# A decoder layer on one core: the q, k and v projections of a token group move partly into the group's own attention steps, at seven matmuls a step instead of eight

## The chip, the core and the metric

The kernel runs on one core of one Trainium2 chip. A core has five engines that run side by side, each with its own queue of instructions that it takes strictly in order: TensorE (PE, matrix multiplies and transposes, with its weight loads shown apart as PEld), VectorE (DVE), ScalarE (ACT), GpSimd (POOL) and SyncE (SP, which here only issues DMA transfers). POOL issues DMAs too. Matrix products land in PSUM, from where DVE or ACT have to copy them out to SBUF.

The metric is the device time of the whole launch in microseconds (us). Before the change it is 601.73 us, the median of three runs (600.86 to 603.8).

## The reference

Eight sequences of 256 tokens, width 512, all in float32. Attention with 16 heads of 32, a decayed running sum over a context, and a feed-forward block whose weights are splines; a layer norm after each.

```python
# attention: per sequence, 16 heads
q, k, v = heads(x @ Wq.T), heads(x @ Wk.T), heads(x @ Wv.T)
q_r, k_r, v_r = q @ Wdown, k @ Wdown, v @ Wdown        # per head, 32 x 32
attn = softmax(q_r @ k_r.T / sqrt(32))
x = layernorm(x + heads_back(attn @ v_r @ Wup) @ Wo.T)
# decayed sum over the sequence: r_t = decay * r_(t-1) + ctx_t * ctx_t
x = layernorm(x + x * r)
# feed-forward; gate_w, up_w, down_w are cubic splines of few control points
x = layernorm(x + (silu(x @ gate_w.T) * (x @ up_w.T)) @ down_w.T)
```

## The kernel before

The 2048 tokens are cut into four groups of 512 (`GT`), each of two sequences (`bb`). All that is heavy is written out by hand in one order: a wrapper (`Ordered`, L299) forces every engine to keep the order of the program. All instructions therefore carry line 308 in the profile, and are told apart by the names of their tiles.

**Start.** The weights are loaded and folded (`Wdown` into `w_q`, `Wup` and `Wdown` into `w_o`), and q, k and v of group 0 are projected in one go (L656 to L659).

**Attention.** The loop at L752 makes 32 steps, one for each group, sequence and quad of four heads. A step issues, in this order: the scores of the *next* step (`scores`, L502, eight small matmuls into four PSUM tiles `sc`), the transposes of three of its four `e` tiles (`tr_e`), two units of other work (`fill(2)`, L819), the fourth transpose, six more units (`fill`, L827), and the product with v (`weighted`, L548, tile `av`). For the next step, DVE takes the row maximum (`nmax`) and ACT the exponential (`e`); DVE and ACT in turn copy the transposes out (`eT`).

**Units.** `units` is a queue of generators with a count each; `fill(n)` (L354) advances the first one n times. A unit is mostly one matmul of 128x128 by 128x512, which the profile shows as two instructions. The kinds are: a projection of one 128-wide quarter of q, k or v of the next group (`project`, L468, four matmuls and an eviction, tiles `ps_q`, `ps_k`, `ps_v`), an output projection (`output`, L571, four matmuls, `ps_o`), and the preparation of the feed-forward inputs of a group (`inputs`, L700, eight units). At the start of a group the twelve projections of the next group join the queue (L756), all q first, then k, then v; they have to be finished before the last step of the group (L771 to L773), after which the next `xT_g` (1 MB) is loaded into the only buffer there is (L775). In the last group nothing is left to project; there `fill(2)` replaces `fill(6)`, and the inputs of the feed-forward's groups 0 and 1 are made (L758 to L760), once the pool `first` (which holds `xT_g`, `w_q`, `w_k`, `w_v`) has been closed.

**Slots.** After every second unit `fill` calls `slot()`, which advances each of the `chains` by one stage, and `some_taps()`. Chains are the layer norms (`norms`, L590, a stage on DVE, ACT or POOL per slot) and the running sum (`recur`, L486). `some_taps` (L442) adds 0.62 to a count and, when it passes one, loads the next of 57 pieces of spline taps through SP and makes weights of the piece before on POOL: six POOL operations for each of the first 16 pieces, three for the rest. The tap buffers are two, so SP waits in its queue for POOL.

**The softmax sums** of a pair of quads go through DRAM in the first three groups: a small transpose, `recT`, a DMA `rd<-recT` and a broadcast DMA `yT<-rd`, both in POOL's queue (L799, L816); DVE multiplies `yT` with `av` in the next step.

**Inputs of the feed-forward.** For a group, `inputs` transposes x2 (four units, tiles `tr_x` and `x2T`) and sends it to DRAM (`xd`, by POOL's queue); then it gathers windows of rows (`xg<-xd`, SP), multiplies with fixed moments (four units, `ps_mom`), copies these to `mom`, writes them to DRAM (`md<-mom`, POOL), and reads them back into the other rows of the same tile (`xg<-md`, SP).

**Feed-forward.** For each group, 32 gate and up products (`pg`, `pu`, `gate_up` L860) on `xg`, then the down products (`y`) and partial sums (`ps_s`). The first products of group 0 follow at once after the last attention step and read `xg` of group 0. The last output projection and its norms run inside this stage (L996, L997).

The lines that the change touches are `fill` (L354), `some_taps` (L442), `project` and `projections` (L468, L482), and the step loop (L754 to L777, L819, L827, L846).

Of the kernel before, what the change touches and what calls it, by code (L numbers as in the profile page):

```python
# [10 lines left out]
F32 = mybir.dt.float32  # L11
# [6 lines left out]
P = 128  # L18
# [3 lines left out]
DC = D // P  # L22
# [3 lines left out]
GT = 512  # L26
NG = NT // GT
# [288 lines left out]
def decoder_kernel(ctx: ExitStack, tc: tile.TileContext, x, xT, ctxT, wq, wkT, wvT, woT, wdownT, wup, decay, up_taps, down_taps, mom_f, sum_f, out, plan):  # L316
# [25 lines left out]
    first = ExitStack()  # L342
    early = first.enter_context(tc.tile_pool(name="early", bufs=1, side="right"))

    nc = Ordered(tc)
    units, chains = [], []

    def slot():

        for c in list(chains):  # L350
            if next(c, c) is c:
                chains.remove(c)

    def fill(n):  # L354

        for i in range(n):
            if units:
                next(units[0][1])
                units[0][2] -= 1
                if not units[0][2]:  # L360
                    units.pop(0)
            if i % 2:
                slot()
                some_taps()

    def norm_plain(h, s, o, other=None):

# [47 lines left out]

    folded, qkvs, rs, sums, xs, yTs = {}, {}, {}, {}, {}, {}
    dram = ctx.enter_context(tc.tile_pool(name="dram", bufs=2, space=bass.MemoryType.DRAM))

    def taps():
# [18 lines left out]
            yield  # L440

    def some_taps():  # L442
        made[0] += 0.62
        while made[0] >= 1:
            made[0] -= 1
            next(weights, None)

    weights, made = taps(), [0]
# [5 lines left out]
    def load_x(g):  # L454
        xT_g = early.tile([P, DC, GT], F32, tag="xT", name="xT_g")
        nc.sync.dma_start(out=xT_g, in_=xT[:, g * GT : (g + 1) * GT].rearrange("(c p) t -> p c t", p=P))
        return xT_g

    def evict_qkv(g, name, m, ps):
        o = qkvs[g]["qkv".index(name)][:, m, :]  # L460
        if name == "q":
            nc.scalar.mul(o, ps, scale)
        elif name == "k":
            nc.vector.tensor_copy(o, ps)
        else:
            nc.scalar.copy(o, ps)

    def project(g, name, m, xT_g):  # L468

        ps = ps_mm.tile([P, GT], F32, tag="mm", name=f"ps_{name}")  # L470
        for c in range(DC):
            if name == "v":
                lhsT, rhs = xT_g[:, c, m * P : (m + 1) * P], folded[name][:, c, :]
            else:
                lhsT, rhs = folded[name][:, c, m * P : (m + 1) * P], xT_g[:, c, :]
            nc.tensor.matmul(ps, lhsT=lhsT, rhs=rhs, start=(c == 0), stop=(c == DC - 1))
            if c < DC - 1:
                yield
        evict_qkv(g, name, m, ps)
        yield  # L480

    def projections(g, xT_g):  # L482
        qkvs[g] = group_tiles(g)
        return [[name, project(g, name, m, xT_g), DC] for name in "qkv" for m in range(DC)]

    def recur(n):  # L486

# [122 lines left out]
    w_v = early.tile([P, DC, D], F32, name="w_v")  # L610
    w_o = last.tile([P, DC, D], F32, name="w_o")
    folded.update(q=w_q, k=w_k, v=w_v)
    xT_g = early.tile([P, DC, GT], F32, tag="xT", name="xT_g")
    for c in range(DC):
        nc.sync.dma_start(out=w_k[:, c, :], in_=wkT[c * P : (c + 1) * P, :])
        nc.scalar.dma_start(out=xT_g[:, c, :], in_=xT[c * P : (c + 1) * P, 0:GT])
# [17 lines left out]
    steps = [(g, bb, quad) for g in range(NG) for bb in range(GT // T) for quad in range(NQ)]  # L634
# [20 lines left out]
        (nc.vector.tensor_copy if m % 2 else nc.scalar.copy)(w_q[:, m, :], ps)  # L655
    for name in "qv":  # L656
        for m in range(DC):
            for _ in project(0, name, m, xT_g):
                pass  # L659
    xT_g = load_x(1)  # L660
    chains.append(recur(0))
    sc = scores(0)
    es = [exponentials(0, j, sc[j]) for j in range(4)]
# [10 lines left out]
    def open_inputs():  # L674
        pool = ctx.enter_context(tc.tile_pool(name="inputs", bufs=1, side="left"))
        ffn["pool"] = pool
        ffn["mom"] = mid.enter_context(tc.tile_pool(name="mom", bufs=1, side="right"))
        ffn["mf"] = pool.tile([P, DC, 2, K2], F32, name="mf")
        nc.sync.dma_start(out=ffn["mf"], in_=mom_f)
# [71 lines left out]
    pending = None  # L751
    for s, (g, bb, quad) in enumerate(steps):  # L752
        n = g * 2 + bb
        if quad == 0 and bb == 0:  # L754
            if g + 1 < NG:
                units += projections(g + 1, xT_g)  # L756
            else:
                first.close()  # L758
                open_inputs()
                units += [["i", inputs(0), 2 * DC], ["i", inputs(1), 2 * DC]]  # L760
        if quad == 0 and n:
            load_rows(n - 1)
            o = [["o", output(n - 1, qc), DC] for qc in range(2)]
            if bb and g + 1 < NG:
                units[1:1] = o[:1]
                units.append(o[1])
            else:
                units[1:1] = o
            chains.append(recur(n))
        more = s + 1 < len(steps)  # L770
        if more and steps[s + 1][0] != g:  # L771
            while any(u[0] != "o" for u in units):
                fill(4)  # L773
            if g + 2 < NG:
                xT_g = load_x(g + 2)  # L775
        if more:
            sc = scores(s + 1)  # L777
        after = []

        def ahead(j):  # L780
# [35 lines left out]
            nc.gpsimd.dma_start(out=y.rearrange("p q t -> p (q t)"), in_=from_)  # L816
        ahead(1)
        eTs.append(evicted(tr2, nc.vector.tensor_copy))
        fill(2)  # L819
        tr3 = transposed(es[3])  # L820
        ahead(2)
        if pending is not None:
# [1 line left out]
            pending = None  # L824
        eTs.append(evicted(tr3, nc.scalar.copy))
        ahead(3)
        fill(6 if g + 1 < NG else 2)  # L827
        if quad % 2 and not short:
            tr = ps_mm.tile([P, 2, T], F32, tag="mm", name="tr_rec")
            for q in range(2):  # L830
# [14 lines left out]
    nc.scalar.activation(neghalf[:, 3:4], neghalf[:, 2:3], AF.Silu)  # L845
    for _ in weights:  # L846
        pass
    mid.close()
    load_rows(NG * 2 - 1)
    units += [["o", output(NG * 2 - 1, qc), DC] for qc in range(2)]  # L850
# [220 lines left out]
```

## Time and profile before

| what | value |
|---|---|
| time, median of three runs | 601.73 us (600.86 to 603.8) |
| the profiled execution: its span from first to last instruction | 599.9 us |
| PE busy | 573.7 us, 96% of the span |
| DVE, ACT, POOL busy | 335.5, 274.3 and 229.3 us |
| mean granted TensorE clock | 0.994 |
| 32 attention steps | from 56.9 us to 399.6 us |
| feed-forward, to the end | 399.6 us to 599.9 us |

Of the profiled execution the page gives the span alone; it stands 1.8 us under the median of the runs, which also count what lies around the first and the last instruction.

How to read it: the page first gives busy time per engine. PE is nearly always busy, so what a change can give or take is read from the places where PE is *not* busy, and from what it waits for there. A line of a timeline gives start and duration in us, engine, operation, the output tile, the input tiles, the shape, how many instructions were merged, and in brackets the idle time of the engine just before and what ended it. A line of a table by stretches gives the stretch, its length, then for each engine the busy time and the count of instructions, the granted clock, and the share and rate of the DMA engines. Ends of matmuls are modelled, and a few matmul records are missing.

### The profile page before, as it was taken

Reading aid. Unit: us, or ns where it says so; the run is one execution under the profiler, and the core shown is the slowest. Engines: PE = TensorE matmul, PEld = TensorE weight load, DVE = VectorE, ACT = ScalarE, POOL = GpSimd, SP = SyncE. Lnnn points to the kernel's source line nnn. Section 1 sums busy time; section 2 is a strip of 40 time slices with the busy share of each in tenths; the row PEclk is TensorE's granted clock in tenths of the full one; section 3 lists DMA queues with packets and bytes.
Section 4 is the critical chain, followed back from the end, with each engine's and each line's share of the span. In section 5 each row is a group of like instructions: output and inputs, shape, how many; then the busy total and the mean of one; then the engine's idle time right before and its main releaser. Section 6 shows DMA issues by size and latency. Waiting matters only on the chain.

```text
span 599.9 us, 9721 instructions
## 1 busy us (share of the span) xinstructions
PE 573.7 (96%) x3327; PEld 289.1 (48%) x3327; DVE 335.5 (56%) x741; ACT 274.3 (46%) x820; POOL 229.3 (38%) x513
## 2 busy tenths in 40 slices
PE   8999999988899999999999899999999999999993
PEld 3544545545455555555555556444344434433432
DVE  0203645558686575786664877776826505714615
ACT  0114644655655645654554677564315314504412
POOL 0000496686554535365440212200361262242253
PEclk9999999999999999999999999999999999999997
DMA  8104134335334115323210564659219987985931
GB/s 289 71 0 153 34 122 144 105 98 174 94 85 158 50 59 176 107 89 124 70 54 2 174 155 109 170 154 213 47 72 248 195 232 179 226 216 135 216 128 70
DMA packets 41696, 77.95 MB, mean 130 GB/s; under 512 B 5952, under 2 KB 10448, under 8 KB 41648
## 3 DMA queue, kind: packets, MB, share of 16 engines
q1 hardware_dynamic: 34576, 62.75, 39.8%
q0 software_dynamic: 6064, 13.41, 6.8%
q10 hardware_dynamic: 1008, 1.18, 0.7%
q8 instruction: 26, 0.43, 0.3%
q14 instruction: 22, 0.18, 0.1%
HBM read 45.22 MB, written 11.12 MB: 94 GB/s over the span
## 4 chain that ended last, share of the span: by engine, by line
PE 77%; DVE 7%; DMA 6%; POOL 5%; issue 2%; ACT 2%; POOLq 0%; SPq 0%; DVEq 0%; ACTq 0%
PE y L308 10%; PE ps_q L308 8%; PE ps_k L308 8%; PE ps_v L308 8%; PE ps_o L308 6%; PE tr_e L308 6%; PE pg L308 5%; PE ps_s L308 5%; PE av L308 5%; PE pu L308 5%; PE sc L308 4%; POOL taps L308 3%; PE ps_mom L308 2%; DMA fin<-sum 2%; DVE nmax L308 2%
## 5 line engine op out<-in xcount | busy, mean ns | idle before, releaser
L308 ACT ACTIVATE e<-sc,nmax 128x256 f32<-128x256 f32 x256 | 120.0, 479 | 76.2 <-DVE nmax L308 76.0
L308 DVE TENSOR_REDUCE nmax<-sc 128x2 f32<-128x512 f32 x128 | 85.2, 682 | 72.0 <-PE sc L308 67.0
L308 POOL TENSOR_TENSOR taps<-taps 128x256 f32<-128x256 f32 (+1 forms) x144 | 87.9, 610 | 33.8 <-DMA taps<-in_down_taps 25.8
L308 PE MATMUL tr_e<-ident,e 128*128 128x128 f32 x512 | 68.0, 276 | 0.8 <-DVE h L308 0.7
L308 PEld LDWEIGHTS tr_e<-ident,e 128*128 128x128 f32 x512 | 57.3, 140 | 22.7 <-issue 19.1
L308 PE MATMUL y<-inter,wd 32*128 32x512 f32 x512 | 63.0, 598 | 0.0
L308 PE MATMUL ps_o<-w_o,yT 128*128 128x512 f32 x128 | 60.0, 600 | 0.3 <-ACT eT L308 0.3
L308 PE MATMUL ps_v<-w_v,xT_g 128*128 128x512 f32 x128 | 58.6, 598 | 0.9 <-DVE eT L308 0.9
L308 PE MATMUL ps_k<-xT_g,w_k 128*128 128x512 f32 x128 | 58.7, 600 | 0.5 <-DMA xT_g<-in_xT 0.5
L308 PE MATMUL ps_q<-xT_g,w_q 128*128 128x512 f32 x128 | 58.2, 596 | 0.9 <-DVE eT L308 0.9
L308 ACT ACTIVATION_READ_ACCUMULATOR e<-sc,nmax 128x1 f32 x256 | 53.1, 207 | 0.0
L308 DVE TENSOR_TENSOR inter<-pu,sg 128x512 f32<-128x512 f32 x64 | 41.2, 687 | 18.3 <-PE pu L308 9.4
L308 POOL TENSOR_TENSOR rs<-va,neghalf 128x1 f32<-128x1 f32 x48 | 28.9, 602 | 49.6 <-DVE va L308 46.9
L308 ACT ACTIVATE sg<-pg 128x512 f32<-128x512 f32 x64 | 37.3, 597 | 18.4 <-PE pg L308 18.4
L308 POOL TENSOR_SCALAR va<-ss 128x1 f32<-128x1 f32 x32 | 6.5, 203 | 100.7 <-ACT x L308 51.1
L308 DVE COPY eT<-tr_e 128x512 f32<-128x512 f32 x64 | 43.8, 684 | 0.8 <-PE tr_e L308 0.7
L308 PEld LDWEIGHTS y<-inter,wd 32*128 32x128 f32 x512 | 26.7, 184 | 32.7 <-issue 27.0
L308 PE MATMUL av<-eT,v_g 128*32 128x256 f32 x512 | 36.7, 385 | 5.0 <-ACT eT L308 2.7
L308 POOL TENSOR_TENSOR r<-r 128x1024 f32<-128x1024 f32 x8 | 15.2, 1895 | 66.0 <-DMA r<-in_ctxT 65.9
L308 ACT COPY eT<-tr_e 128x512 f32<-128x512 f32 x64 | 37.3, 583 | 2.4 <-PE tr_e L308 2.4
L308 PE MATMUL sc<-k_g,q_g 32*128 32x256 f32 x512 | 37.4, 401 | 0.2 <-ACT e L308 0.2
L308 PEld LDWEIGHTS ps_v<-w_v,xT_g 128*128 128x128 f32 x128 | 23.1, 190 | 26.0 <-issue 24.3
(106 smaller groups left out, 739.8 us busy)
## 6 DMA issues: line engine op xcount, KB each, us to landing
nat<-inter SPq DMA_DIRECT2D x64, 256.0 KB
taps<-in_down_taps SPq DMA_DIRECT2D x40, 256.0 KB
taps<-in_up_taps SPq DMA_DIRECT2D x16, 384.0 KB
xg<-xd SPq DMA_DIRECT2D x8, 616.0 KB
r<-in_ctxT SPq DMA_DIRECT2D x8, 512.0 KB
x_t<-in_x SPq DMA_DIRECT2D x16, 256.0 KB
fin<-sum POOLq DMA_DIRECT2D x16, 256.0 KB, 5.3
out<-h SPq DMA_DIRECT2D x16, 256.0 KB
```

The lines of the kernel that those rows point to most:

```text
L308: return lambda *a, **k: self.tc.keep_in_program_order(f(*a, **k))
```

## The change

The projections of group g+1 are no longer bound to be finished within group g. They are queued in the order in which the steps will need them (`ORDER`: q0, k0, v0, v1, q1, k1, q2, k2, q3, k3, v2, v3), and a new function `require` advances the queue, without slots, until a named projection has been made; it is called for q and k of a step before its scores, and for two quarters of v before the product with v. Each step of the first three groups now takes seven units (2 and 5) instead of eight, each step of the last group six (2 and 4) instead of four. The number of slots is given to `fill`: one and three in a step of the first three groups, as before; one and two in the last group, where there were one and one. The count of taps grows by 0.66 a slot, not 0.62. `xT` of the next group is loaded when the last projection of a group has been evicted. The pool `first` is closed, and the preparation of the feed-forward's inputs queued, in the fifth step of the last group, not in its first. The places at which output projections enter the queue change as well. The sum of matmuls is the same.

```diff
-    def fill(n):
+    def fill(n, slots=None):
+        slots = n // 2 if slots is None else slots
         for i in range(n):
...
-            if i % 2:
+            if (i + 1) * slots // n > i * slots // n:
                 slot()
                 some_taps()
+
+    def require(g, *names):
+        while any(u[0] == (g, name) for u in units for name in names):
+            fill(1, 0)
...
+    ORDER = [(name, int(m)) for name, m in ("q0", "k0", "v0", "v1", "q1", "k1", "q2", "k2", "q3", "k3", "v2", "v3")]
...
     def some_taps():
-        made[0] += 0.62
+        made[0] += 0.66
...
-    def project(g, name, m, xT_g):
+    def project(g, name, m):
+        xT_g = xTs[g]
...
         evict_qkv(g, name, m, ps)
+        if g and (name, m) == ORDER[-1] and g + 1 < NG:
+            xTs[g + 1] = load_x(g + 1)
         yield
...
-    def projections(g, xT_g):
+    def projections(g):
         qkvs[g] = group_tiles(g)
-        return [[name, project(g, name, m, xT_g), DC] for name in "qkv" for m in range(DC)]
+        return [[(g, f"{name}{m}"), project(g, name, m), DC] for name, m in ORDER]
...
-    xT_g = load_x(1)
+    xTs[1] = load_x(1)
...
-        if quad == 0 and bb == 0:
-            if g + 1 < NG:
-                units += projections(g + 1, xT_g)
-            else:
-                first.close()
-                open_inputs()
-                units += [["i", inputs(0), 2 * DC], ["i", inputs(1), 2 * DC]]
+        if quad == 0 and bb == 0 and g + 1 < NG:
+            units += projections(g + 1)
         if quad == 0 and n:
             load_rows(n - 1)
             o = [["o", output(n - 1, qc), DC] for qc in range(2)]
-            if bb and g + 1 < NG:
-                units[1:1] = o[:1]
-                units.append(o[1])
-            else:
-                units[1:1] = o
+            at = 2 if units and (bb == 0 or units[0][2] < 2) else 1
+            units[at:at] = o[:1]
+            units[at + 2 : at + 2] = o[1:]
             chains.append(recur(n))
         more = s + 1 < len(steps)
-        if more and steps[s + 1][0] != g:
-            while any(u[0] != "o" for u in units):
-                fill(4)
-            if g + 2 < NG:
-                xT_g = load_x(g + 2)
         if more:
+            g1, _, quad1 = steps[s + 1]
+            require(g1, f"q{quad1}", f"k{quad1}")
             sc = scores(s + 1)
+        if quad == 0 and bb and g + 1 == NG:
+            require(g, *(f"{name}{m}" for name, m in ORDER))
+            first.close()
+            open_inputs()
+            units += [["i", inputs(0), 2 * DC], ["i", inputs(1), 2 * DC]]
...
-        fill(2)
+        fill(2, 1)
         tr3 = transposed(es[3])
...
-        fill(6 if g + 1 < NG else 2)
+        if g + 1 < NG:
+            fill(5, 3)
+        else:
+            fill(4, 2)
+        require(g, f"v{bb * 2}", f"v{bb * 2 + 1}")
...
     for _ in weights:
         pass
+    while units:
+        fill(2)
     mid.close()
```

## The prediction

> **What bounds the kernel now.** I read the page's busy times first, then PE by stages, then what PE waited for, then the queues that end those waits.
>
> ```profile
> span 599.9 us, 9721 instructions
> ```
>
> Stages from the table by stretches (stretch, length, then PE busy first): steps of group 0, 1, 2, 3.
>
> ```profile
> 56.87:143.88 87.01, 83.63 (x502) 44.74 (x501) 48.43 (x91) 46.80 (x165) 58.58 (x110) 1.00 0.38 118
> 143.88:236.00 92.12, 90.37 (x525) 48.00 (x525) 63.64 (x139) 50.61 (x174) 47.06 (x86) 1.00 0.37 112
> 236.00:327.80 91.80, 90.94 (x536) 48.48 (x535) 61.91 (x142) 50.49 (x172) 40.14 (x73) 1.00 0.24 74
> 327.80:399.60 71.80, 65.58 (x511) 37.52 (x510) 55.16 (x131) 46.33 (x154) 15.71 (x25) 1.00 0.56 142
> ```
>
> PE sets the pace: it is idle 3.4, 1.8, 0.9 and 6.2 us, 12.2 us in all. The change leaves PE's work as it is (in the chain of waits four projection instructions, two matmuls, take 1.72 us, so 0.86 a matmul; a step of eight units takes 11.08, one of seven 10.22). So it can win at most these 12.2 us, and loses whatever new waits it makes. The waits of PE in group 3, and the timeline around the worst one of group 0:
>
> ```profile
> PE av L308 <- DVE x2T L308: 2.3, 2, 1.2
> PE av L308 <- ACT eT L308: 1.3, 2, 1.0
> PE tr_rec L308 <- DVE mom L308: 0.8, 1, 0.8
> PE ps_mom L308 <- DVE mom L308: 0.8, 1, 0.8
> ```
> ```profile
> 123.84 0.57 POOL L308 TENSOR_TENSOR rs<-va,neghalf 128x1 f32<-128x1 f32 x1
> ...
> 124.44 0.95 DVE L308 TENSOR_SCALAR x<-h,nm,rs 128x512 f32<-128x512 f32 x1 [4.79 <-POOL rs L308]
> ...
> 126.89 1.09 PE L308 MATMUL tr_e<-ident,e 128*128 128x128 f32 x8 [0.66 <-DVE h L308]
> ...
> 128.87 1.98 PE L308 MATMUL ps_v<-w_v,xT_g 128*128 128x512 f32 x4 [0.88 <-DVE eT L308]
> ```
>
> In group 0 a norm's `rs` sits in POOL's queue behind tap work; DVE, in order, stands 4.79 us at `x`, and PE, whose transposes need PSUM that DVE should free, loses 0.66 + 0.88 = 1.54 us. Third view, POOL between its softmax DMAs, and SP and PE around the feed-forward's inputs:
>
> ```profile
> 95.21 0.74 POOL L308 DMA_DIRECT2D yT<-rd  x1 [1.92 <-DMA rd<-recT]
> ...
> 107.80 1.26 POOL L308 TENSOR_TENSOR taps<-taps 128x256 f32<-128x256 f32 x2 [2.08 <-DMA taps<-in_up_taps]
> ...
> 116.09 0.52 POOL L308 DMA_DIRECT2D rd<-recT  x1
> ```
> ```profile
> 341.79 1.53 SPq L308 DMA_DIRECT2D xg<-xd  x4
> 354.98 1.72 SPq L308 DMA_DIRECT2D xg<-md  x2
> ```
> ```profile
> 342.38 1.94 PE L308 MATMUL ps_mom<-x2T,mf 128*64 128x512 f32 x8
> ```
>
> POOL had no idle time ahead of 116.09: it is already late there. And from the last moment product of a group (344.3) to the *issue* of the read-back into `xg` pass 10.7 us.
>
> **The change, part by part.** I followed the queue by hand, counting units.
>
> *Removed.* Before, the 48 matmuls and one 8-matmul output pair of group 0 fill seven steps and the eighth has no unit: it waits 0.27 + 1.35 = 1.62 us for ACT. After, 56 units fill eight steps of seven exactly. In group 3 the four steps with outputs wait 0.35 + 0.99 + 0.29 = 1.63 us for `eT`; two more matmuls (1.7 us) cover that. Gain 3.25 us. The steps with inputs waited 4.4 us (of the 6.2) on evictions by DVE and ACT; after, these units come in rows of four as before, or denser: zero, between -1.5 and +2. The collisions of groups 1 and 2 (2.6 us): DVE has 62 us of work in 92, after 62 in 85; zero, between -2 and +2.5. Slots per step stay; in groups 0 to 2 no `require` has anything to force.
>
> *POOL in group 0.* Between the softmax DMAs of steps 3 and 5 POOL now has six pieces, not five (0.66 for 0.62; the counts reach 7.9 and 13.2), each 3.24 us (95.97 to 99.21), plus 1.9 for `r`, plus the 2.08 wait for a transfer: 23.4 us. Two shorter steps give 20.4 where they gave 22.1. Step 5 starts at 56.9 + 5x10.22 + 0.7 (the first step is longer by 0.7) = 108.7, its `rd` is wanted 2 us later, at 110.6; POOL comes free near 116.7, 6 us late (before: 1.7). Then 4.2 us of DMA pair, one piece, and `va`, `rs`: done near 125, when it was done at 124.4 before, although PE would start step 6 at 118.9 instead of 124.5. Behind the waiting DVE instruction stand `nmax` and the `eT` copies, and PE has one PSUM buffer left (`av`, `tr_r` and the begun `ps_o` hold three). Full price: 1.54 becomes 7.5, so +6. Low end: -1.5, the wait of before gone. POOL's schedule rests on one rounding and one transfer, so I take +4.5.
>
> *xT.* v3, the last of its group, is now followed closely by q0. Group 1 to 2: `tr_rec` 0.5, `av` 1.0, scores 1.1, transposes 1.5, 4.1 us in all. Group 2 to 3: four output matmuls and a transpose, 3.9. Before, the load was issued at 229.11, just after its last reader, and its 1 MB moved at 400 GB/s from 230.9 to about 233.7: 4.6 us after. Each costs 0.5 to 0.7 us, +1.2; between 0 and +3 (SP is behind POOL in its tap waits by some us in group 0).
>
> *The feed-forward's inputs.* The queue of group 3 holds 16 matmuls of projections, outputs of n = 5 and 6, then inputs(0) and inputs(1): the last start in step 29 of 0 to 31, where they started in step 24. inputs(0)'s last moment product is the fourth of six units of step 30. From there to the first gate product: two `tr_x` with a wait (1.3), `av` 1.0, and step 31 without scores: transposes 1.7, two `tr_x` with wait 1.7, `tr_e` 0.8, four moment units with wait 4.4, `tr_rec` 0.5, `av` 1.0: about 12.4 us. The gate product needs `xg` whole: copy to `mom`, POOL's `md` DMA, its landing, SP's read-back. Issue 10.7 us after the last moment product (11.1 for group 1: 381.5 to 392.6), and of that second one data moved until about 398.3, 5.7 us later: 17 us. PE stands 17 - 12.4 = 4.6; I take +4.5. Low end 0 (at the shortest `md` landing, 3.6 us, and no `xd` traffic), high end 9 (`xd` of inputs(1), 1 MB, in the same engines). Nothing else is in PE's program order there: the last output comes after the gate products. Before, 55 us of steps covered this (344.3 to 399.6).
>
> *Clock.* At the start of the span three idle products of 512, 512 and 256 columns, 2.15 us by the row above, took 4.20, so the clock was low after rest; at the end it was 1.00 in 590:592 and 0.54 in 592:594, with PE's last matmul at 590.4.
>
> ```profile
> 1.44 4.20 PE L308 MATMUL ps_idle<-idle 128*128 128x512 f32 x6 [1.44 <-DVE idle L308]
> ```
>
> So a wait of several us may cost up to 2.05 more. The longest before, 1.74, shows none (1.00). For the two long waits I take +1 each, between 0 and 2.05.
>
> Sum: -3.25 + 4.5 + 1.2 + 4.5 + 2 = +8.95 us, on a span of 599.9. The median stands 1.8 above the span, which the change doesn't touch: 601.73 + 8.95 = 610.7 us.
>
> Two rules of the Trainium skill. "DMA: Bandwidth & Descriptors", section on the anatomy of one DMA (POOL's path), puts a transfer at about 2.0 us fixed plus bytes over 436 GB/s; for the 640 KB of the write, and taken for the read-back too, that is an estimate of 3.5 us each, `xg` would be whole before PE asks, and the sum 5.5 us less, 605.2. The trace disagrees: landing of `md` has a median of 5.7 us and the read-back 5.7, in a busy queue, and I go by it. "TensorE: Matmul & The Clock Gate", Part 1, lets the clock halve after an idle window of about 3.4 us and restores it after one busy window: 1.7 us for each long wait, 3.4 for the 2 in my sum, so 612.1; the drop within 1.8 us of the last matmul fits a window that runs free.
>
> **The rivals.** (1) Only one of the two long waits comes: POOL keeps up (for: group 0 of before has 6.3 us of POOL idle at 64.3), or `xg` is whole in time (for: the shortest landing). Either way 5.5 us less: 605.2. (2) Neither comes, but the xT loads do: -3.25 + 1.2, 599.7, no change to be measured. (3) Faster: PE always has a unit at hand, so that DVE's lateness is covered in all steps and all 12.2 us of idle go; against it, the two xT loads (1.2) and the wait for `xg` (5.5 with clock) remain: 601.7 - 12.2 + 6.7 = 596.2. Its place is steps 4 to 7; it decides once POOL's lateness costs PE under about 2 us. (4) The xT load is caught in SP's queue behind a wait for POOL; SP's longest for `wu` was 13.1 us, less 4 of cover: +8 on the sum, 619.
>
> **How the numbers follow.** Forecast 0.45, with its own range of 605 to 616; one long wait only 0.25; none 0.10; faster 0.12; SP 0.08. A measurement here tells 0.5% (3 us) from no change, so under 598.7 is faster and over 604.7 slower. Slower: all but a trace of the forecast, a good half of (1), and (4): 0.66. Same: the rest of (1) and (2): 0.20. Faster 0.14. The range leaves out most of (3) below and (4) above: 598.5 to 617.
>
> **What would show it.** Right: steps of 10.2 us in groups 0 to 2; a PE wait of some us in step 6 (near 120 us) ended by DVE behind POOL's `rs`; two waits under 1 us of `ps_q` for the xT load; the first `pg` after a wait of 3 to 9 us for `xg<-md`, with a dip of the clock; the sum of PE's idle in the attention near 20 us. Wrong: no gap ahead of the first `pg`, or POOL idle ahead of step 5's `rd`. The forecast fails most easily if the transfers of `md` land fast in an emptier queue.

## The result: 650.9 us, and the profile after

The changed kernel takes 650.88 us (median of four runs, 649.03 to 653.94), against 601.39 us for the kernel before: a ratio of 1.082, with a 95% interval of 1.079 to 1.086. That is 49.5 us slower. The forecast had the sign, +9 us, and its range ended at 617. The span of the profiled execution grew as the median did, from 599.9 to 648.9 us.

The page's first lines, the kernel after:

```profile
span 648.9 us, 9726 instructions
## 1 busy us (share of the span) xinstructions
PE 583.7 (90%) x3327; PEld 296.1 (46%) x3327; DVE 335.6 (52%) x741; ACT 275.0 (42%) x820; POOL 232.4 (36%) x513
```

DVE, ACT and POOL are busy as long as before, within about 3 us. PE has the same matmuls and is still busy for 10.0 us more (583.7 for 573.7): matmuls at half clock take longer. The other 39 us are idle time of PE. The table by stretches of the kernel after, the steps of groups 0 to 3 (stretch, length, busy time of PE, PEld, DVE, ACT and POOL, granted clock, DMA share and rate):

```profile
56.70:157.90 101.20, 86.95 (x512) 46.15 (x511) 51.62 (x102) 48.63 (x171) 64.50 (x119) 0.95 0.31 97
157.90:249.70 91.80, 84.73 (x523) 45.37 (x519) 62.35 (x142) 49.89 (x172) 46.78 (x84) 1.00 0.38 118
249.70:349.60 99.90, 88.59 (x527) 46.76 (x523) 61.81 (x142) 49.96 (x172) 38.66 (x69) 0.95 0.27 77
349.60:436.70 87.10, 76.43 (x533) 42.67 (x529) 61.34 (x148) 49.80 (x159) 16.99 (x27) 1.00 0.26 74
```

Lengths have to be compared with the work that each group now holds. Those of the kernel before are taken in the same way, from the first scores issued in a group (at 56.87, 144.87, 237.03 and 328.82) to those of the next, and to the first gate product at 399.58; the prediction's stretches of groups 1 to 3 begin some 1 us earlier. Groups 1 and 2 have eight matmuls fewer than before (6.9 us at 0.86 each), group 3 has sixteen more (13.7 us).

| stage | before | after | difference | difference for the same work |
|---|---|---|---|---|
| group 0 | 88.0 | 101.2 | +13.2 | +13.2 |
| group 1 | 92.2 | 91.8 | -0.3 | +6.6 |
| group 2 | 91.8 | 99.9 | +8.1 | +15.0 |
| group 3 | 70.8 | 87.1 | +16.3 | +2.6 |
| feed-forward | 200.3 | 212.2 | +11.9 | +11.9 |

So the loss is in five places at once, and for the same work no stage gained. What PE waited for, over the whole span of the kernel after (total us, times, longest):

```profile
PE tr_e L308 <- DVE eT L308: 21.2, 21, 9.2
PE ps_s L308 <- DMA nat<-inter: 7.9, 1, 7.9
PE ps_q L308 <- DMA xT_g<-in_xT: 7.1, 2, 5.8
PE tr_e L308 <- ACT eT L308: 5.1, 7, 0.7
PE pg L308 <- issue: 3.2, 2, 2.6
```

None of these five groups came to 1 us before. Each is one mechanism, or two in the case of `tr_e`; I take them in the order of the program.

**POOL in group 0.** The timeline around step 6, POOL's softmax DMAs, the norm behind them, and PE:

```profile
120.89 0.52 POOL L308 DMA_DIRECT2D rd<-recT  x1
124.53 0.72 POOL L308 DMA_DIRECT2D yT<-rd  x1 [3.12 <-DMA rd<-recT]
128.91 0.57 POOL L308 TENSOR_TENSOR rs<-va,neghalf 128x1 f32<-128x1 f32 x1
129.51 0.94 DVE L308 TENSOR_SCALAR x<-h,nm,rs 128x512 f32<-128x512 f32 x1 [10.82 <-POOL rs L308]
131.71 1.11 PE L308 MATMUL tr_e<-ident,e 128*128 128x128 f32 x4 [9.25 <-DVE eT L308]
```

This is the chain that the prediction described, and larger: `rd` was wanted near 111.6 (an estimate: 2 us after step 5 began at 109.7) and issued at 120.89, 9 us late where 6 were forecast; DVE stands 10.82 us at `x`, PE 9.25 us behind DVE. Step 6 lasts 24.05 us.

**Steps that begin with a half-made tile.** The other `tr_e` waits are short and many. PE's timeline in step 1 and in steps 14 and 15:

```profile
68.83 1.04 PE L308 MATMUL tr_e<-ident,e 128*128 128x128 f32 x8
70.22 0.66 PE L308 MATMUL tr_e<-ident,e 128*128 128x128 f32 x4 [0.35 <-DVE eT L308]
...
226.13 0.66 PE L308 MATMUL tr_e<-ident,e 128*128 128x128 f32 x4 [0.79 <-DVE eT L308]
227.52 0.66 PE L308 MATMUL tr_e<-ident,e 128*128 128x128 f32 x4 [0.73 <-ACT eT L308]
...
239.88 0.66 PE L308 MATMUL tr_e<-ident,e 128*128 128x128 f32 x4 [1.53 <-DVE eT L308]
```

A projection is four matmuls into one PSUM tile. Eight units a step are two whole projections; seven are not, so most steps now end with a tile that has one to three of its four matmuls. As I read the program, that tile keeps one of the four buffers of `ps_mm`, from which the transposes `tr_e`, the norms' `tr_r`, the output products and `av` are taken too; the third transpose (in steps 6, 7, 14, 15, 22 and 23, where norms take buffers too, already the second) then has no buffer until DVE has copied the first one out, which is what the trace names as the end of the wait. Of the 24 steps of groups 0 to 2, the six that begin with no open tile are steps 0, 4, 8, 12, 16 and 20 (28 matmuls are seven whole tiles). None of the six has a `tr_e` wait; each of the other eighteen has one. The lengths of the steps say the same (the other steps of groups 0 to 2 are like these, but for steps 6 and 17 with their long waits, and step 23 with 14.42 us in part at half clock):

| steps of groups 0 to 2 | length, us |
|---|---|
| 0, 4, 8, 12, 16, 20 (no open tile) | 10.95, 10.21, 11.53, 10.17, 10.16, 10.16 |
| 1, 2, 3, 5 (open tile) | 10.62, 10.60, 10.61, 11.05 |
| 9, 10, 11, 13, 14, 15 (open tile) | 10.61, 11.05, 11.30, 11.05, 12.99, 13.13 |

(Step 0 is longer by 0.7 us, as the prediction had it, and step 8 has 1.30 us of the next paragraph in it.) Apart from these two, the forecast's 10.2 us holds in the aligned steps and nowhere else.

**The xT load.** PE's first product of each of groups 2 and 3, SP's issue of the second load, and the stretches in which it moved, the kernel after:

```profile
161.82 1.96 PE L308 MATMUL ps_q<-xT_g,w_q 128*128 128x512 f32 x4 [1.30 <-DMA xT_g<-in_xT]
...
273.66 2.90 PE L308 MATMUL ps_q<-xT_g,w_q 128*128 128x512 f32 x3 [5.80 <-DMA xT_g<-in_xT]
```
```profile
264.02 0.38 SPq L308 DMA_DIRECT2D xT_g<-in_xT  x1
```
```profile
264.00:268.00 4.00, 3.86 (x12) 1.55 (x11) 2.47 (x5) 3.09 (x12) 2.30 (x4) 1.00 0.61 190
268.00:272.00 4.00, 0.00 (x0) 0.00 (x0) 1.84 (x5) 0.81 (x2) 0.00 (x0) 0.88 0.97 220
```

PE could start 5.2 us after the first load's issue at 156.57, and 9.6 us after the second's. While the second load was under way all transfers together moved 190 to 220 GB/s, the engines being 97% busy in the second row; the kernel before had 398 GB/s at 232:236, while its load moved. POOL's broadcast DMA `yT<-rd` had been issued 0.2 us ahead of it, at 263.82, and a piece of taps 0.5 us behind it. Which of them slowed the load, or whether either did, was not tried.

**The feed-forward's inputs.** SP's queue and PE at the end of the attention, the kernel after:

```profile
430.31 1.73 SPq L308 DMA_DIRECT2D xg<-md  x2
...
433.63 5.91 SPq L308 DMA_DIRECT2D xg<-xd  x4
442.01 1.53 SPq L308 DMA_DIRECT2D xg<-md  x2
...
445.16 24.18 SPq L308 DMA_DIRECT2D nat<-inter  x16
```
```profile
436.69 1.09 PE L308 MATMUL pg<-xg,wg 64*128 64x512 f32 x2 [2.60 <-issue]
...
478.71 8.18 PE L308 MATMUL ps_s<-nat,sf 128*64 128x512 f32 x28 [7.94 <-DMA nat<-inter]
```

The first gate product waits 2.60 us, and another 0.64 at its second pair: the place was forecast, with 4.5. The profile names no releaser here (`issue`); that it is `xg` follows from the program, the read-back `xg<-md` having been issued 6.4 us earlier, and from e3 below. The 7.94 us at `ps_s` were not forecast. SP's reads of group 1's inputs (at 433.63 and 442.01) stand ahead of the 16 gathers `nat` in SP's queue, which are issued from 445.16 on, 8.5 us after the first gate product. Before, the last read of these inputs had been issued at 392.58, 7 us ahead of the end of the attention, and SP went straight to the gathers, 2.8 us after the first gate product:

```profile
402.38 13.37 SPq L308 DMA_DIRECT2D nat<-inter  x16
```

**The clock.** The table by stretches of 4 us around two of the places, the kernel after (the granted clock is the third number from the end):

```profile
124.00:128.00 4.00, 0.00 (x0) 0.00 (x0) 0.00 (x0) 0.00 (x0) 3.21 (x6) 0.96 0.14 43
128.00:132.00 4.00, 0.29 (x2) 0.30 (x3) 2.49 (x4) 0.91 (x4) 3.51 (x9) 0.50 0.40 121
132.00:136.00 4.00, 3.27 (x10) 2.00 (x9) 0.94 (x2) 1.61 (x7) 3.61 (x9) 0.50 0.37 98
136.00:140.00 4.00, 3.64 (x10) 1.62 (x9) 1.86 (x6) 0.00 (x0) 2.93 (x7) 0.76 0.17 66
```
```profile
336.00:340.00 4.00, 1.99 (x18) 1.30 (x11) 2.66 (x6) 2.12 (x8) 0.32 (x1) 0.91 0.25 88
340.00:344.00 4.00, 4.00 (x13) 2.22 (x12) 3.24 (x9) 0.41 (x2) 0.00 (x0) 0.66 0.00 0
```

After the wait of step 6 the clock is at half for 10.2 us (0.3 + 4 + 4 + 1.9, from the four rows), for the last six of which PE is at work again (from 131.71). The mean over the span falls from 0.994 to 0.972.

### The profile page after: what moved, and what is told of

Its sections match the earlier page's. It is cut to its first block, busy times and chain, and to the rows that moved or that the text cites. A ratio compares the mean times of both kernels' runs of the same rounds, so it can differ in the third digit from the quotient of the medians.

```text
span 648.9 us, 9726 instructions
## 1 busy us (share of the span) xinstructions
PE 583.7 (90%) x3327; PEld 296.1 (46%) x3327; DVE 335.6 (52%) x741; ACT 275.0 (42%) x820; POOL 232.4 (36%) x513
## 4 chain that ended last, share of the span: by engine, by line
PE 67%; DVE 11%; DMA 10%; POOL 6%; ACT 3%; issue 3%; SPq 0%; POOLq 0%; DVEq 0%; ACTq 0%
PE y L308 8%; PE ps_v L308 7%; PE ps_o L308 7%; PE ps_q L308 7%; PE tr_e L308 6%; PE ps_k L308 6%; PE pg L308 5%; PE ps_s L308 5%; PE pu L308 4%; POOL taps L308 4%; PE sc L308 3%; PE av L308 3%; DVE nmax L308 2%; DMA xT_g<-in_xT 2%; DMA fin<-sum 2%
## 5 line engine op out<-in xcount | busy, mean ns | idle before, releaser
L308 POOL TENSOR_TENSOR taps<-taps 128x256 f32<-128x256 f32 (+1 forms) x144 | 89.9, 625 | 27.7 <-DMA taps<-in_down_taps 20.6
L308 PE MATMUL tr_e<-ident,e 128*128 128x128 f32 x512 | 75.2, 282 | 26.4 <-DVE eT L308 21.2
L308 PE MATMUL ps_q<-xT_g,w_q 128*128 128x512 f32 x128 | 62.2, 619 | 7.1 <-DMA xT_g<-in_xT 7.1
L308 PE MATMUL ps_o<-w_o,yT 128*128 128x512 f32 x128 | 61.3, 609 | 0.0
L308 ACT ACTIVATE sg<-pg 128x512 f32<-128x512 f32 x64 | 37.3, 597 | 23.8 <-PE pg L308 22.5
L308 PE MATMUL pg<-xg,wg 64*128 64x512 f32 x128 | 40.6, 613 | 3.2 <-issue 3.2
L308 PE MATMUL pu<-xg,wu 64*128 64x512 f32 x128 | 39.8, 604 | 0.0
L308 PEld LDWEIGHTS ps_q<-xT_g,w_q 128*128 128x128 f32 x128 | 23.9, 199 | 31.4 <-issue 28.5
```

The lines of the kernel that those rows point to most:

```text
L308: return lambda *a, **k: self.tc.keep_in_program_order(f(*a, **k))
```

## The experiments

The theory after these readings: the loss has four separate causes, POOL's lateness in group 0 (A), the open tiles (B), the single xT buffer (C) and the late inputs with SP's order behind them (D), and the half clock follows from the waits. The rival: there is one cause, the shorter step of seven units, in which DVE and ACT are simply too slow, and the waits are where it happens to show. The first four kernels take away one cause each from the kernel after. Ratios are to the kernel before, with 95% intervals; "gain" is against the 650.9 us of the kernel after. The intervals leave about 3 us either way in a gain.

**e1_aligned: whole projections in every step (B).** Steps take 8, 8, 8 and 4 units in place of 7, 7, 7 and 7.

```diff
-        if g + 1 < NG:
-            fill(5, 3)
+        slots = 3 if g + 1 < NG else 2
+        few = quad == 3 if g + 1 < NG else quad % 2
+        if few:
+            fill(2, 2)
+            if slots == 3:
+                slot()
+                some_taps()
         else:
-            fill(4, 2)
+            fill(6, slots)
```

> The changed kernel with the same number of units over four steps (28) but in whole projections: steps of 8, 8, 8 and 4 units in groups 0 to 2, and 8 and 4 in turn in group 3, so that no projection's PSUM tile stays open from one step into the next. In the changed kernel every step that begins with an open tile (18 of 18) has a PE wait of tr_e for eT, none of the others has. Theory A (an open tile takes one of four PSUM buffers from the transposes): these waits, 15 us outside steps 6 and 7, go; 12 to 16 us less than the changed kernel, about 637. Rival (DVE has too much work for a shorter step, 62 us in 85): the mean step is the same, so the waits stay; within 3 us of 650.9.

Measured: 628.37 us, ratio 1.045 (1.040 to 1.050), a gain of 22.5. More than the 12 to 16 expected. Whole projections also end the last use of the `xT` buffer at the end of step 16, so that the second load is issued 7.5 us ahead of the product that needs it (at 247.52, for 254.97) and is no longer waited for; group 2 gains 14.0 us where group 1 gains 5.7. Step 6, too, falls from 24.05 to 20.50 us. So this run mixes B and part of C; e10 below prices B by itself.

**e2_taps: fewer taps per slot in group 0 (A).** The count grows by 0.5 a slot in group 0, and by 0.66 after.

```diff
 def some_taps():
-        made[0] += 0.66
+        made[0] += rate[0]
...
-    weights, made = taps(), [0]
+    weights, made, rate = taps(), [0], [0.5]
...
+        rate[0] = 0.5 if g == 0 else 0.66
```

> The changed kernel with the tap count at 0.5 a slot in group 0 and 0.66 after it, so that POOL has four pieces, not six, between the softmax DMAs of steps 3 and 5. Theory A (POOL late, DVE stands 10.8 us behind its rs, PE 9.25 us behind DVE, then a low clock): the wait in step 6 goes with what hangs on it; 12 to 15 us less than the changed kernel, about 637. Rival (the wait is of PSUM, or of the load of r in SP's queue): at most 3 us less.

Measured: 641.51 us, ratio 1.066 (1.063 to 1.068), a gain of 9.4. The timeline of POOL and PE in steps 5 and 6:

```profile
111.54 0.52 POOL L308 DMA_DIRECT2D rd<-recT  x1 [1.31 <-ACT recT L308]
...
119.61 0.57 POOL L308 TENSOR_TENSOR rs<-va,neghalf 128x1 f32<-128x1 f32 x1
...
123.17 0.66 PE L308 MATMUL tr_e<-ident,e 128*128 128x128 f32 x4 [0.78 <-DVE eT L308]
```

POOL now waits for ACT ahead of `rd`, where it was 9 us late, `rs` comes 9.3 us earlier, and step 6 falls from 24.05 to 13.00 us. The 0.78 us that stay are those of an open tile. The total is below the 12 to 15 us expected: step 15 now takes 14.59 us for 13.13 with waits of the same kind, and the feed-forward 213.4 for 212.2. The mechanism of A stands.

**e3_inputs: both inputs ahead of the output products of the last sequences (D).**

```diff
-            units += [["i", inputs(0), 2 * DC], ["i", inputs(1), 2 * DC]]
+            units[0:0] = [["i", inputs(0), 2 * DC], ["i", inputs(1), 2 * DC]]
```

> The changed kernel with inputs(0) and inputs(1) queued ahead of the output pair of n = 6 in step 28, not behind it. Theory A (both waits at the start of the feed-forward come from the late end of the inputs: 3.2 us of pg for xg, and 7.9 us of ps_s for nat, whose transfers stand in SP's queue behind the read-back of inputs(1)): both go, with the low clock after them; 12 to 15 us less than the changed kernel, about 637. Rival (nat waits for bandwidth of the DMA engines): only the first goes, 3 to 6 us less.

Measured: 636.41 us, ratio 1.057 (1.054 to 1.060), a gain of 14.5. PE has no wait ahead of its first gate product, and 2.8 us at `ps_s` in place of 7.9. D stands, within the 12 to 15 us expected.

**e4_xt2: two buffers for xT (C).** The next load starts a whole group earlier. (`bd_down` moves to another pool to make room.)

```diff
-        xT_g = early.tile([P, DC, GT], F32, tag="xT", name="xT_g")
+        xT_g = early.tile([P, DC, GT], F32, tag="xT", name="xT_g", bufs=2)
...
-        if g and (name, m) == ORDER[-1] and g + 1 < NG:
-            xTs[g + 1] = load_x(g + 1)
...
+            if g + 2 < NG:
+                xTs[g + 2] = load_x(g + 2)
```

> The changed kernel with two buffers for xT, the load of group g+2 issued at the start of group g (a 64 KB constant moves to another pool to make room). Theory A: the two waits of ps_q for xT, 1.3 and 5.8 us, go, and the low clock after the second (2.6 us); 7 to 10 us less than the changed kernel, about 642. Rival (the early load pushes tap pieces back in SP's queue, and POOL falls behind in group 0 instead): no gain, or up to 5 us more.

Measured: 644.62 us, ratio 1.070 (1.067 to 1.073), a gain of 6.3, a little under the 7 to 10 expected. Both waits are gone and step 17 falls from 18.68 to 10.61 us. PE's product that had waited 5.80 us:

```profile
266.13 1.88 PE L308 MATMUL ps_q<-xT_g,w_q 128*128 128x512 f32 x4
```

**e5_eight: the changed kernel with eight units a step.** If seven is the trouble, eight should give most of the time back.

```diff
-            fill(5, 3)
+            fill(6, 3)
```

> The changed kernel with eight units a step again in groups 0 to 2 (2 and 6), all else as changed: the order of the projections, the late inputs, six units in group 3, 0.66. Eight units are two whole projections, so no tile stays open, v3 of a group ends a step or more before q0 of the next, and the step gives POOL 11.1 us, not 10.2. Theory A (the losses hang on the seven, but for the late inputs): the 15 us of open tiles, the 7 us of xT with clock and a good part of step 6's 13 us go, the waits at the start of the feed-forward stay; about 620, between 614 and 626. Rival (the order of the projections and the new places of the outputs cost by themselves): over 635.

Measured: 637.82 us, ratio 1.061 (1.058 to 1.063). The theory's number is missed by 18 us, and the total lies where the rival put it, over 635, although the open tiles are gone (`tr_e` behind DVE's `eT` is 2.2 us in all, from 21.2). With eight a step the queue is empty too soon: by the end of group 2 all projections have been made, the inputs, queued in step 28 behind an output pair, still start in step 29, and steps 25 to 27 have nothing to put beside their softmax. PE's timeline there, and the stretch behind its longest wait:

```profile
358.87 1.05 PE L308 MATMUL av<-eT,v_g 128*32 128x256 f32 x10 [1.09 <-ACT eT L308]
...
368.03 1.91 PE L308 MATMUL av<-eT,v_g 128*32 128x256 f32 x10 [3.18 <-ACT eT L308]
...
378.11 1.05 PE L308 MATMUL av<-eT,v_g 128*32 128x256 f32 x10 [2.12 <-ACT eT L308]
```
```profile
368.00:372.00 4.00, 3.97 (x27) 1.88 (x28) 2.77 (x15) 1.69 (x6) 0.55 (x1) 0.50 0.00 0
```

Group 3 takes 82.8 us for work that took 70.8, 2.7 us of the xT wait remain, and the feed-forward's 11.9 us are untouched. So the number of units a step cannot be judged by itself: the late inputs make a queue that lasts to the end necessary, and seven is what stretches it so far. Against the rival, that the new order costs by itself, speaks e7 below, which keeps that order and is no slower than the kernel before.

**e6_before66: the kernel before, with 0.66 taps a slot.** Is the tap count alone to blame for POOL?

```diff
-        made[0] += 0.62
+        made[0] += 0.66
```

> The kernel before with the tap count at 0.66 a slot and nothing else changed: POOL gets six pieces between the softmax DMAs of steps 3 and 5 in place of five, in steps of 11.1 us. Theory A (POOL's lateness in group 0 comes from the count and the shorter step together): one of the two makes POOL some 3 us later than before at step 5, and PE's wait in step 6 grows from 1.5 to between 3 and 6 us; 2 to 6 us slower than the kernel before. Rival (the shorter step alone did it): within 1 us of it.

Measured: 602.77 us against 601.13, ratio 1.0020 (1.0006 to 1.0033): +1.6 us (1.2 by the ratio, 0.4 to 2.0), below the 2 to 6 us of the theory and about at the limit of 1 us set for the rival. Step 6 grows by 2.4 us (12.87 to 15.25), and the next steps give some back. In steps of eight units POOL nearly keeps up with 0.66; put together with e2, it is the shorter step with the higher count that puts it 9 us behind. Seven units with a count of 0.62 were not tried.

**e3b_inputs0: only group 0's inputs ahead.** Which of the two inputs causes which wait?

```diff
-            units += [["i", inputs(0), 2 * DC], ["i", inputs(1), 2 * DC]]
+            units[0:0] = [["i", inputs(0), 2 * DC]]
+            units.append(["i", inputs(1), 2 * DC])
```

> The changed kernel with only inputs(0) ahead of the output pair of n = 6, inputs(1) last as in the change. Theory A: xg of group 0 is whole in time and the 3.2 us wait of pg goes, but SP still stands behind the read-back of inputs(1) when the first nat is to leave, so the wait of ps_s for nat stays, 5 to 9 us; 3 to 7 us less than the changed kernel, about 646. Rival (the wait for nat hangs on the late inputs(0) or on bandwidth alone): it falls to under 3 us as with both ahead; 636 or so.

Measured: 646.67 us, ratio 1.075 (1.073 to 1.077). The total is the expected one and the split is not. The wait at `ps_s` fell to 2.4 us instead of staying, and a gate product waits instead, behind ACT's `sg`:

```profile
442.10 2.56 PE L308 MATMUL pg<-xg,wg 64*128 64x512 f32 x4 [5.94 <-ACT sg L308]
```

A right total with wrong parts shows nothing of the mechanism that was expected. ACT's timeline names what holds this product:

```profile
441.45 1.08 ACT L308 ACTIVATE sg<-pg 128x512 f32<-128x512 f32 x2 [7.79 <-DMA md<-mom]
```

The first `sg` stands until the write `md<-mom` of group 1's moments has landed, and PE, which by the program may run four tiles ahead, stands behind it. The program gives a reason, which was not tried: the tile `mom` lies in a pool that is closed just ahead of the pool of `sg`, so `sg` can get the memory that `md<-mom` still reads. This is a third effect of the late inputs. It is in the kernel after too, where the first `sg` starts at 442.17, 0.16 us after SP's read-back that waits for the same write, and the gathers, which need its results, can't start earlier; the profile shows no idle time of PE itself there. With both inputs ahead (e3) `sg` starts 1.2 us after the first gate product.

**e8_reads: the reads of group 1's inputs put off.** The kernel before already puts off the reads of the later groups until their feed-forward needs them. Here group 1 joins them; nothing else differs from the kernel after.

```diff
-        if b > 1:
+        if b > 0:
...
-                if b > 1:
+                if b > 0:
```

> The changed kernel with the window and moment reads of inputs(1) put off until the gate products of group 0 are issued, as the kernel does for groups 2 and 3; nothing else moves, and the same bytes are moved. Theory A (the first nat stood in SP's queue behind these reads): the 7.9 us wait of ps_s for nat and the low clock after it go, the wait of pg for xg stays; 8 to 12 us less than the changed kernel, about 641. Rival (the DMA engines are short of bandwidth there): the nat wait stays above 4 us, at most 4 us less.

Measured: 641.42 us, ratio 1.066 (1.063 to 1.069), a gain of 9.5. SP's queue:

```profile
442.39 12.78 SPq L308 DMA_DIRECT2D nat<-inter  x16
...
457.13 8.82 SPq L308 DMA_DIRECT2D xg<-xd  x4
465.99 1.62 SPq L308 DMA_DIRECT2D xg<-md  x2
```

The 16 gathers are issued in 12.8 us, not 24.2, the 7.9 us wait is gone, and the wait for `xg` of group 0 stays (3.3 us). The same bytes move, a little later, and the first `sg` is as late as before (441.04, 7.19 us behind `md<-mom`). So the 7.9 us were a matter of the order in which SP issues, and a wait separate from that of the first gate product. The DMA engines are full in both kernels while the gathers move (a share of 1.00 from 444 to 472 in the kernel after, 1.05 from 444 to 464 here), so what the reads cost ahead of the gathers is their place before them in the queue and in the engines; the run doesn't part the two.

**e7_all: e1, e2, e3 and e4 together.**

> The changed kernel with all four: whole projections in a step, 0.5 a slot in group 0, both inputs ahead of the last output pair, two xT buffers. Theory A (the four places are separate and are the whole loss): gains of 22.5, 9.4, 14.5 and 6.3 us add up, less the xT wait that two of them share (8 us); 650.9 - 52.7 + 8 = 606, between 598 and 610, with PE idle in the attention near 15 us or less and the mean granted clock at 0.99 again. Rival (they share a cause, and what one gives back another takes): over 618.

Measured: 601.34 us against 601.13, ratio 1.0001 (0.9991 to 1.0011). The four edits give back all of the 49.5 us; taken singly, their gains add up to 52.7 (22.5 + 9.4 + 14.5 + 6.3), part of the excess being the xT wait that e1 and e4 both remove. The clock's mean is 0.995 and PE's busy time 572.4 us, so the 10 us of slow matmuls went with the waits.

**e10_not_aligned: e7 without the alignment.** The clean price of B: POOL on time, xT early, inputs early, and still seven units a step.

```diff
-        slots = 3 if g + 1 < NG else 2
-        few = quad == 3 if g + 1 < NG else quad % 2
...
+        if g + 1 < NG:
+            fill(5, 3)
+        else:
+            fill(4, 2)
```

> The four repairs but one: seven units a step as in the change (2 and 5, in the last group 2 and 4), so projections stay open from step to step; taps, inputs and xT as repaired. Theory A: what an open PSUM tile costs by itself, the 15 us of eT waits counted in the changed kernel outside step 6 and some more where they let the clock fall; 601.3 + 14 to 20, about 618. Rival (the aligned steps won so much only because they also hid the xT load and helped POOL): under 610.

Measured: 619.52 us, ratio 1.029 (1.027 to 1.032), 18.2 us over e7. PE's waits in this kernel, and the same line of e7:

```profile
PE tr_e L308 <- DVE eT L308: 14.8, 22, 2.1
PE tr_e L308 <- ACT eT L308: 5.1, 7, 0.7
```
```profile
PE tr_e L308 <- DVE eT L308: 0.7, 2, 0.3
```

The 19.9 us of these two groups, against 0.7, are about the price. It is not all theirs: e7 has 6.1 us of waits of projections behind DVE's `eT`, in its long steps, and e10 has none of these. Counted by ratios, each against the kernel before of its own session, the price is 17.5 us. The two kernels have the same units, slots and taps overall; only where a step ends in a projection differs. With e7 equal to the kernel before, that speaks against the rival too: an average of seven units a step costs nothing if projections aren't cut.

**e11_before_offset: the kernel before, shifted by one matmul.** One extra unit is taken at the start of each of the first three groups. All steps keep their eight units, but each begins with an open tile.

```diff
+        if quad == 0 and bb == 0 and g + 1 < NG:
+            fill(1)
```

> The kernel before with one unit more at the very start of each of the first three groups and nothing else: eight units a step, but every step of these groups then begins with a projection one matmul old and its PSUM tile open. No step is shorter, no load or order moves. Theory A (the open tile is the cause, not the shorter step): waits of tr_e for eT of 0.3 to 0.4 us in odd steps, and more in the two steps where a norm's transposes hold a buffer too; 6 to 15 us slower than the kernel before. Rival (the shorter step is the cause): within 2 us of it.

Measured: 609.85 us against 601.74, ratio 1.013 (1.010 to 1.015), +8.1 us. The wait group, and one instance in step 1:

```profile
PE tr_e L308 <- DVE eT L308: 9.6, 23, 0.9
```
```profile
72.20 0.66 PE L308 MATMUL tr_e<-ident,e 128*128 128x128 f32 x4 [0.35 <-DVE eT L308]
```

The same 0.35 us as in the changed kernel, now in a step of eight units (11.47 us, from 11.08). So the open tile is enough by itself and needs no shorter step. That the transpose is held for want of a buffer is read from the program (four `ps_mm` buffers, one kept); a fifth buffer was not tried, `ps_mm` and `ps_big` having four each.

**e9_best: e7 with the put-off reads of e8.** e7 ends its attention earlier than the kernel before (397.3 for 399.6 us) and loses it again to 2.4 us at `ps_s`.

> All four repairs, and the put-off reads of inputs(1). With the four alone the attention ended 2.3 us earlier than in the kernel before (first pg at 397.3, not 399.6), and 2.4 us were lost again to ps_s waiting for nat. Theory A: that wait goes; 2 to 4 us less than with the four, 597 to 600, a small gain over the kernel before. Rival (the put-off reads collide with the nat transfers and xg of group 1 comes late): 601 or more.

Measured: 598.62 us (598.4 to 599.18) against 601.74, ratio 0.9946 (0.9929 to 0.9962), the fastest of all. The first gate product, with no wait, in place of 399.58 before:

```profile
396.31 1.13 PE L308 MATMUL pg<-xg,wg 64*128 64x512 f32 x4
```

## Why the prediction was right or wrong

The accounting, from the runs: open tiles 18.2 us (e10 against e7), POOL in group 0 9.4 (e2), late inputs and SP's order 14.5 (e3), the xT loads 6.3 (e4), 48.4 of the 49.5 us. Each gain includes the half clock that its waits brought. The four were not taken from one and the same kernel, and each carries some us of noise, so that they come out so near the whole is in part chance; that the four together are the whole rests on e7.

- **"So it can win at most these 12.2 us."** No run won more. The gain forecast for what is removed was 3.25 us. The waits of `av` for ACT's `eT`, 2.7 us before, are gone from the kernel after, and e9, in which the four causes are gone, wins 3.1 (601.74 to 598.62): for the same work its group 0 is 2.9 us shorter than before, group 3 1.5, groups 1 and 2 1.4 longer together. The places were right. That the total agrees to 0.15 us is luck, since e9 also has waits of its own and SP's reads in another order.
- **"The collisions of groups 1 and 2 ... zero, between -2 and +2.5."** Here the prediction failed. For the same work, group 1 lost 6.6 us and group 2 15.0, of which 1.3, and 5.8 with some low clock, are the xT loads. I divided DVE's 62 us of work by a stretch of 85 and took the ratio for the risk; PE's waits come from PSUM buffers, whose number I used in step 6 only ("PE has one PSUM buffer left") and nowhere else. Counting seven units against projections of four would have given the six aligned steps. In place of zero the runs showed 18 us for the open tiles in all groups (e10 against e7), 18 of the 40 us that were missed.
- **POOL, +4.5, full price 6.** The mechanism was right link by link, and the term mis-sized: 9.25 us of wait, and 11 us of step 6 by e2. POOL issued `rd` at 120.89, not near 116.7. Some 2.4 us of that lie ahead of the six pieces: in step 3, POOL issued `rd` without a pause behind tap work, and it took 3.03 us to come back, not 1.92. Some 1.7 us lie in the pieces, of which a few took up to 1.9 us for 1.26. The one wait for a transfer that was counted, 2.08 us, came, as 2.20 us for the load of `r`.
- **The xT loads, +1.2, at most 3.** Right in place and too small: 1.30 and 5.80 us. The cover was as counted (PE ran 4.0 and 3.8 us before it stood, for 4.1 and 3.9). The landing was not: I took the 4.6 us of the load before for both, and they took 5.2 and 9.6.
- **The wait for `xg`, +4.5, between 0 and 9.** Near: 3.24 us, at the first gate product. The estimate of 3.5 us a transfer that I had drawn from the Trainium skill ("DMA: Bandwidth & Descriptors", the anatomy of one DMA) would have left no wait there; this run has one, so the landing times of the profile were the better guide.
- **"Nothing else is in PE's program order there."** True, and not enough. I followed PE's order and not SP's: the 16 gathers that the later `ps_s` needs stand in SP's queue behind group 1's reads: 7.9 us, and 9.5 us with what hangs on it (e8). The prediction followed POOL's queue piece by piece and costed SP's at nothing here.
- **The clock, +2.** PE was busy for 10 us more. Two long waits were priced at one short stretch each; the stretches measured were 10.2 us after step 6 and 6.8 after the second xT wait (granted clock 0.88, 0.50 and 0.77 in the rows of 4 us from 268 to 280), and more of them elsewhere.
- **The rivals and the signs.** None of the rivals happened. Of the signs of being right, the wait in step 6 and the wait ahead of the first `pg` came; steps of 10.2 us came only where no tile was open, and PE was idle in the attention for 43.3 us (380.0 less 336.7), not near 20. Rival 3's condition, POOL's lateness under 2 us, holds in e7 and e9, which then end at 601.3 and 598.6, not at 596.2; they differ from the change in more than that.

## What to carry to other kernels

If filler work is cut into units, let every step take whole accumulation groups: a tile left open across a step boundary keeps a PSUM buffer from the step's own tiles, and one matmul's shift cost 8 us here and seven units for eight 18. If a piece of work is moved later, walk through every in-order queue that it issues into, and ask what stands *behind* it in each: PE stood 3.2 us for the moved inputs themselves and 7.9 us for SP's gathers behind them. And judge a small change of a tuned rhythm with its supports: an average of seven units a step was no slower than eight once taps, buffers, order and cuts fitted it.

## What the runs showed of the hardware

The clock fell without a long wait. Around 338 us of the kernel after, PE's two longest waits were 1.28 and 0.73 us, and PE was busy for 2.0 of the 4 us of the row at 336:340; still the granted clock was at half for 3.4 us (0.7 + 2.7, from the two rows shown above). At step 6 it stayed at half for some six us after PE had begun to work again. The stretches measured were 3.4, 6.8 and 10.2 us long, multiples of 3.4. The Trainium skill's page "TensorE: Matmul & The Clock Gate", Part 1, tells of an activity window of about 3.4 us that runs free: the lengths agree with it. What it gives as a condition, a whole idle window, doesn't describe the stretch at 339, where PE was partly busy.

The same 1 MB load, by the same instruction and queue, took 4.6 us (before), 5.2 and 9.6 us. Around the slow one all transfers together moved 190 to 220 GB/s, with a broadcast read from DRAM and a piece of taps issued within 0.5 us of it; around the load before, 398.
